# Two graph layers on one core: the second layer's first 21 gathers moved ahead of the first layer's last three groups

## The chip, the cores and the metric

The kernel runs on one core of a Trainium2 chip. The metric is the device time of one execution in microseconds (us); it was measured in three runs, and the median is given. Engines are named as in the profile: PE is TensorE (PEld its weight loads), DVE VectorE, ACT ScalarE, POOL GpSimd, SP SyncE; POOLq, ACTq and SPq are their instruction queues, which also issue DMAs.

## The reference

A graph has 6250 nodes with 256 features each and 106250 edges (a source, a destination, one of two relations), sorted by destination; each node also has an edge to itself. All is float32.

```python
# layer one
msgs = where(rel == r, edge_nn(x[src], W_rel[r], b_rel[r]))       # two dense layers with relu
agg = segment_sum(msgs, dst)
gates = agg @ W_ih.T + b_ih + b_hh
i, f, g, o = split(gates, 4)
hn = sigmoid(o) * tanh(sigmoid(i) * tanh(g))
x = layernorm(x + relu(relu(hn @ W1.T + b1) @ W2.T + b2) @ W3.T + b3)
# layer two: graph attention, 4 heads of 64
h = x @ W
e = leaky_relu(a_src[src] + a_dst[dst], 0.2)
alpha = exp(e - segment_max(e, dst)); alpha /= segment_sum(alpha, dst)
y = segment_sum(h[src] * alpha, dst) + bias + x
x = layernorm(x + relu(layernorm(y) * gamma + beta))
```

Layer two's gather of h[src] needs rows of h that layer one makes last, for any destination: that is the one barrier in the middle of the program.

## The kernel before

*Prelude.* The edge lists are read and packed so that self edges are left out (100000 edges stay), and turned into index tables: `idx0` and `idx1` hold, for each tile of 128 edges, the row that each lane gathers in layer one and in layer two. Beside this TensorE makes the messages of every node for both relations, which are stored in the table `parts0` (L1138 to L1179).

*Tiles, windows, groups.* The edges are 782 tiles of 128 (`TC`). Seven tiles are a window (`WT`, 112 windows, `NW`), whose destinations lie in at most 64 consecutive nodes (`SLOTS`); two windows are a group (56 groups, `NG`), which fills the 128 partitions with nodes. `low_i` and `low_b` hold the first node of each window.

*Layer one* (L1611 to L1675). A loop over steps n: step n issues the gather of one tile from `parts0` on POOL (`gather`, L1270, L1657) and, four steps later (`LAG`), the product that adds this tile into its group's sum in PSUM (`sum0`, L1621). What follows a sum, `turn` (L1433) and `update` (L1461), is written as generators; `Steps.step` (L1287) runs each up to its next `yield` once a step, so the order of instructions on every engine is fixed by hand, and a piece of group g stands on its engine behind the sums of later groups. `update` runs the gates and the three dense layers for four groups at a time, for single groups at the end (`quads`, L1310). It makes the row of layer two, `hr` (256 values of h and 4 logits, L1572), and stores it to `rows1` on SP (L1580); the last group's rows go there by a scatter on POOL (L1582). After the last step, `run.finish` (L1675) runs what is left.

*Layer two* (L1678 to L1975). A like loop: step t gathers one tile from `rows1` (L1946). Gathered tiles lie in ten buffers of seven tiles (`ring` "G", 10), which both layers share, so at most 70 tiles are ahead of their use. ACT copies the logits out (L1968, L1960); `weights` (L1751) then takes a pair of groups (single groups at the end) and finds maxima by transposing the logits on PE (L1766) and scanning them on DVE (L1773 to L1785); `weighted` (L1806) multiplies the rows by the exponentials (L1818), which frees a gather buffer; `sum1` (L1899) adds them up by one-hot products on PE (L1927); `finish` (L1825) normalizes and stores. `ahead` (L1699) loads a pair's tables on the ACT queue (L1708, L1715). The first pair's weights are started when tile 28 has come.

*Waits.* Each engine works its instructions in order. A gather waits until its buffer is free and, in layer two, until all stores to `rows1` have landed.

Of the kernel before, what the change touches and what calls it, by code (L numbers as in the profile page):

```python
# [42 lines left out]
P = 128  # L43
N = 6250
# [18 lines left out]
def blocks_of(n, size):  # L63
    return [(i, min(size, n - i)) for i in range(0, n, size)]
# [10 lines left out]
NC = -(-EC // CT)  # L75
HA = D + H
LAG = 4
SORTED = "the fast path runs only where the chip has found the edges sorted"


# [623 lines left out]
def gnn_kernel(  # L704
# [37 lines left out]
    rows1 = dram.tile([NP + P, HA], F32, name="rows1")  # L742
    slots = dram.tile([NW, (WT + 1) * P], BF16, name="slots")
    cuts = dram.tile([(NC + 1) * CT, P], F32, name="cuts")
    kept = dram.tile([NG, P, 3 * D], F32, name="kept")
    packed = dram.tile([2 * BLOCKS, HB], I32, name="packed")

# [19 lines left out]
    mark = const.tile([P, COLS], BF16, name="fmark")  # L767
    tail_i = const.tile([P, 1], I32, name="tail_i")
    tail_x = const.tile([P, 1], I32, name="tail_x")


    with (
# [15 lines left out]
        with (  # L788
# [257 lines left out]
            dstE = lp.tile([P, COLS], F32, name="dstE")  # L1046
            src0 = src1
            nc.vector.tensor_scalar(src0[:CT], src1[:CT], 1.0, None, op0=OP.subtract)
            for to, of in (
                (idx0, row),  # L1050
                (dstE, list_f[:, :, 1:]),
                (mark, rel_f[:, :, :P]),
                (idx1, src0),
                (first, steps),
            ):
                for k0, kn in blocks_of(NC, 4):
                    pt = lps.tile([P, 4 * CT], F32, name="turned")
                    for k in range(kn):
                        nc.tensor.transpose(
                            pt[:, k * CT : (k + 1) * CT], of[:CT, k0 + k, :], ident[:CT, :CT]  # L1060
                        )
                    n = min(kn * CT, COLS - k0 * CT)
                    if to is not mark:
                        nc.vector.tensor_copy(to[:, k0 * CT : k0 * CT + n], pt[:, :n])
                        continue

                    to2, of2 = (
                        ap.rearrange("p (g j) -> p g j", j=2 * WT)
                        for ap in (mark[:, k0 * CT : k0 * CT + n], pt[:, :n])
                    )  # L1070
                    for a, b, c in ((0, 1, 0), (1, 2, WT), (2, WT + 1, 1), (WT + 1, 2 * WT, WT + 1)):
                        nc.vector.tensor_copy(to2[:, :, a:b], of2[:, :, c : c + b - a])
# [50 lines left out]
            nc.vector.tensor_scalar(tail_x, tail[:, 0:1], float(NP - 1), None, op0=OP.min)  # L1123


            for w0, wn in blocks_of(NW, P // (WT + 1)):
                pt = lps.tile([P, 4 * CT], F32, name="turned")
                n = wn * (WT + 1)
                nc.tensor.transpose(
                    pt[:n, :P], slot[:, w0 : w0 + wn, :].rearrange("p w j -> p (w j)"), ident  # L1130
                )
                rel_b = lp.tile([P, P], BF16, name="rel_b", bufs=2)
                nc.scalar.copy(rel_b[:n, :], pt[:n, :P])
                nc.sync.dma_start(
                    slots[w0 : w0 + wn, :].rearrange("w (j e) -> (w j) e", e=P), rel_b[:n, :]
                )
# [51 lines left out]
    with tc.If(odd_v == 0) as cmp:  # L1188
        fast(
            tc, x, WihT, bih, bhh, W1T, b1, W2T, b2, W3T, b3, Wg, att_src, att_dst, bias, gamma,  # L1190
            beta, out, parts0, rows1, slots, cuts, kept, iota_f, iota_p, ident, idx0, idx1,
            first, mark, slot, low_i, tail_i, tail_x,
        )
    with cmp.Else():
        general(
# [6 lines left out]
def fast(  # L1202
# [32 lines left out]
    low_i,  # L1235
    tail_i,
    tail_x,
):

    nc = tc.nc  # L1240
# [27 lines left out]
        )[1]  # L1268

    def gather(to_tile, table, idx):  # L1270
        nc.gpsimd.indirect_dma_start(  # L1271
            out=to_tile,
            out_offset=None,
            in_=table,
            in_offset=bass.IndirectOffsetOnAxis(ap=idx, axis=0),
        )
# [24 lines left out]
    def half_of(w):  # L1301
        return slice(SLOTS * (w % 2), SLOTS * (w % 2 + 1))
# [20 lines left out]
    node3 = keep.tile([P, NG, 2, 3, 2 * H], BF16, name="node3")  # L1323
    nc.vector.memset(node3, 0.0)
    loop = keep.tile([P, NG, H], F32, name="loop")
    vec = keep.tile([P, 2, D], F32, name="fvec")
    eps_c = keep.tile([P, 1], F32, name="eps_c")
    nc.vector.memset(eps_c, EPS)
# [32 lines left out]
    def in_order(done, g):  # L1361
        if g != len(done):
            raise ValueError("groups are out of order")
        done.append(g)


    with (
# [32 lines left out]
        for k, v in enumerate((gamma, beta)):  # L1400
# [2 lines left out]
        nc.sync.dma_start(  # L1403
            rows1[N:, :].rearrange("(p r) f -> p (r f)", r=2),
            zero[: (NP + P - N) // 2, : 2 * HA],
        )

        run = Steps()
# [24 lines left out]
        def turn(g, i, ps, aT):  # L1433

            agg = ring(up, [P, D], F32, "agg", 3)

            kind = ring(up, [P, 2], F32, "kind", 3)
            for r in range(2):
                nc.vector.tensor_scalar(  # L1439
                    kind[:, r : r + 1], ps[:, D:], float(3 - r), None, op0=OP.is_equal  # L1440
                )
            for r, of in ((0, ps[:, :D]), (1, agg)):
                nc.vector.scalar_tensor_tensor(  # L1443
                    agg,
                    loop0[g][:, r * D : (r + 1) * D],
                    kind[:, r : r + 1],
                    of,
                    op0=OP.mult,
                    op1=OP.add,
                )  # L1450
            yield 1
            pt = ring(upp, [P, 4 * P], F32, "fpg", 5)[:, : 2 * P]
            for k in range(2):
                nc.tensor.transpose(  # L1454
                    pt[:, k * P : (k + 1) * P], agg[:, k * P : (k + 1) * P], ident
                )
            nc.vector.tensor_copy(  # L1457
                aT[:, :, i * P : (i + 1) * P], pt.rearrange("p (k n) -> p k n", k=2)
            )

        def update(groups, aT):  # L1461
            slow = min(3, max(1, (NG - 4 - groups[0]) // 4))
# [102 lines left out]
            for i, g in enumerate(groups):  # L1565
                u = everyone
                ph = ring(upp, [P, 4 * P], F32, "fpg", 5)[:, : D + 2 * H]
                for k in range(2):
                    nc.tensor.matmul(
                        ph[u, :], hs[i][:, k, u], Wx[:, k, :], start=(k == 0), stop=(k == 1)  # L1570
                    )
                hr = ring(up, [P, D + 2 * H], F32, "hr", 4)  # L1572
                nc.scalar.copy(hr[u, :], ph[u, :])  # L1573
                nc.scalar.copy(keep3[i][u, 2, :], ph[u, :D])

# [1 line left out]
                for w in windows_of(g):  # L1577
                    if w in at_w:
                        to = rows1[bass.ds(at_w[w], SLOTS), :]
                        nc.sync.dma_start(to, hr[half_of(w), :HA])  # L1580
                if g == NG - 1:
                    nc.gpsimd.indirect_dma_start(  # L1582
                        out=rows1,
                        out_offset=bass.IndirectOffsetOnAxis(ap=tail_i, axis=0),
                        in_=hr[:, :HA],
                        in_offset=None,
                    )
                yield 1
                nc.sync.dma_start(kept[g, u, :], keep3[i][u, :, :].rearrange("p c f -> p (c f)"))

# [53 lines left out]
        for n in range(TC + LAG):  # L1644
            if n < TC:
                g, t = order[n]
                k, turns = n % WT, n // WT // 10 % 2
                if k == 0:
                    seven = ring(rowsp, [P, WT * HA], F32, "G", 10).rearrange(
                        "p (j f) -> p j f", f=HA  # L1650
                    )
                    m = min(WT, TC - n)
                    of, to = mark[:, n : n + m, None], seven[:, :, D : D + 1]
                    nc.scalar.copy(to[:, ::-1, :][:, :m, :] if turns else to[:, :m, :], of)

                got[t] = seven[:, WT - 1 - k if turns else k, : D + 1]
                gather(got[t][:, :D], parts0, idx0[:, t : t + 1])  # L1657
                if t == order_of(g)[0]:
                    ohs[g] = ring(ep, [P, 2 * W8, SLOTS], F32, "oh0", 2)
                    one_hot(ohs[g], 2 * g, 2 * W8)  # L1660
                    loop0[g] = ring(up, [P, 2 * D], F32, "loop0", 2)
                    own_rows(g, lows_of(windows_of(g)), loop0[g], loops)
                    if g == NG - 1:
                        rows_x[g] = ring(up, [P, D], F32, "fxn", 8)
                        own_rows(g, {}, rows_x[g], x)
            if n >= LAG:
                g, t = order[n - LAG]
                if t != 2 * WT * g:
                    sum0(g, t, t == TC - 1)
                elif g:  # L1670
                    sum0(g - 1, t, True)
                if t == 2 * WT * g + WT:
                    sum0(g, 2 * WT * g)
            run.step()
        run.finish()  # L1675


    with (  # L1678
# [10 lines left out]

        nc.scalar.preload_act_table_set("natural_log_exp_and_others")  # L1690
        run = Steps()
        G, late = {}, []

        def tiles_in(g):

# [241 lines left out]
        run.start(aheads())  # L1937
        t = 0
        while t < TC + LAG or late or queue or run.chains:
            if t < TC:  # L1940
                w = t // WT
                if t % WT == 0:
                    G[w] = ring(rowsp, [P, WT * HA], F32, "G", 10).rearrange(
# [2 lines left out]
                gather(G[w][:, t - WT * w, :], rows1, idx1[:, t : t + 1])  # L1946
            k = t - LAG
            if 0 <= k < TC:
                w = k // WT
                g = w // 2  # L1950
                pair = pair_of[g]
# [86 lines left out]
```

## Time and profile before

| what | us |
|---|---|
| median of 3 runs | 2273.53 |
| lowest and highest | 2273.02, 2274.97 |
| profiled execution | 3062.77 |
| its span | 3061.0 |
| first gather of layer one | 203.84 |
| last gather of layer one, first of layer two | 1434.05, 1482.51 |
| last gather of layer two | 2969.30 |
| busy: PE, DVE, POOL | 1529.9, 1229.8, 1527.2 |
| one gather on POOL | 0.95 |

The profiled execution is 789 us longer than the timed runs, so its stretches cannot be read as stretches of these; what one operation takes, and what waits for what, can.

How to read the lines: a group of instructions gives line, engine, operation, what it writes and reads, and the count; after the first bar the busy time and the mean of one in ns; after the second the idle time of the engine before them and what ended most of it. A line of the order of time gives start, duration, engine, line, operation; in brackets the idle time of its engine before it, and what released it ("issue": nothing that the profile shows; "remote": a semaphore whose setter it cannot tell). A line of waits gives total us, times, and the longest. A line of stretches gives its length, the busy time and count for PE, PEld, DVE, ACT and POOL, and then the granted share of the PE clock, the DMA share and GB/s.

### The profile page before, as it was taken

Reading aid. Unit: us, or ns where it says so; the run is one execution under the profiler, and the core shown is the slowest. Engines: PE = TensorE matmul, PEld = TensorE weight load, DVE = VectorE, ACT = ScalarE, POOL = GpSimd, SP = SyncE. Lnnn points to the kernel's source line nnn. Section 1 sums busy time; section 2 is a strip of 40 time slices with the busy share of each in tenths; the row PEclk is TensorE's granted clock in tenths of the full one; section 3 lists DMA queues with packets and bytes.
Section 4 is the critical chain, followed back from the end, with each engine's and each line's share of the span. In section 5 each row is a group of like instructions: output and inputs, shape, how many; then the busy total and the mean of one; then the engine's idle time right before and its main releaser. Section 6 shows DMA issues by size and latency. Waiting matters only on the chain. (4 is left out here: it accounts for less than half of the span.)

```text
span 3061.0 us, 22029 instructions
## 1 busy us (share of the span) xinstructions
PE 1529.9 (50%) x5722; PEld 792.0 (26%) x5722; DVE 1229.8 (40%) x3333; ACT 506.0 (17%) x1526; POOL 1527.2 (50%) x1603
## 2 busy tenths in 40 slices
PE   9871276767676756788223332423324233242344
PEld 5540132323233322334111111212112121121222
DVE  8240132322333233333114544535445354453656
ACT  3320011211121211134201111111111111111112
POOL 0227566666666666641473354553545545455440
PEclk9985688878788878889555665656656566565667
DMA  4343334444444434442342243342433334243330
GB/s 150 109 137 108 96 104 122 143 124 139 132 139 135 131 118 132 131 127 79 100 117 79 80 116 86 103 108 81 117 84 106 105 83 117 82 111 100 88 99 27
DMA packets 163393, 332.53 MB, mean 109 GB/s; under 512 B 42451, under 2 KB 74290, under 8 KB 163257
## 3 DMA queue, kind: packets, MB, share of 16 engines
q0 software_dynamic: 75968, 208.00, 24.6%
q1 hardware_dynamic: 64736, 82.92, 8.4%
q10 hardware_dynamic: 22553, 40.12, 4.3%
q8 instruction: 47, 0.77, 0.1%
q14 instruction: 89, 0.73, 0.1%
HBM read 278.79 MB, written 52.12 MB: 108 GB/s over the span
## 5 line engine op out<-in xcount | busy, mean ns | idle before, releaser
L1271 POOL DMA_INDIRECT G<-rows,fidx x782 | 743.9, 951 | 746.6 <-DVE gw L1818 513.3
L1271 POOL DMA_INDIRECT G<-parts,fidx x782 | 752.3, 962 | 483.9 <-issue 216.4
L1927 PE MATMUL fps<-gw,oh 128*64 128x264 f32 (+1 forms) x1674 | 448.2, 480 | 284.1 <-DVE gw L1818 218.1
L1633 PE MATMUL fps<-G,oh 128*64 128x257 f32 (+1 forms) x1674 | 465.2, 428 | 91.5 <-issue 49.7
L1927 PEld LDWEIGHTS fps<-gw,oh 128*64 128x64 f32 (+1 forms) x1674 | 233.9, 171 | 468.6 <-DVE gw L1818 231.7
L1818 DVE TENSOR_TENSOR gw<-G,bank 128x1792 f32<-128x1792 f32 (+1 forms) x167 | 249.1, 1491 | 169.8 <-issue 123.7
L1633 PEld LDWEIGHTS fps<-G,oh 128*64 128x64 f32 (+1 forms) x1674 | 204.1, 152 | 332.1 <-issue 219.8
L1777 PE MATMUL turn<-s,toward 120*120 120x1 f32 (+2 forms) x60 | 15.7, 331 | 435.9 <-DVE s L1774 432.4
L1486 PE MATMUL fpg<-faT,fWihT 128*128 128x512 f32 (+2 forms) x432 | 182.9, 549 | 49.2 <-issue 28.7
L1773 DVE TENSOR_TENSOR_SCAN s<-cut,turn 120x128 f32<-120x128 f32 (+2 forms) x30 | 12.6, 419 | 448.1 <-remote 442.6
L1439 DVE TENSOR_SCALAR kind<-fps 128x1 f32<-128x1 f32 x112 | 12.4, 152 | 359.6 <-PE fps L1633 183.8
L1454 PE MATMUL fpg<-fident,agg 128*128 128x128 f32 x112 | 29.2, 351 | 236.7 <-DVE agg L1443 132.7
L1354 DVE TENSOR_TENSOR oh<-bank,fslot 128x1024 f32<-128x1024 f32 x112 | 136.1, 1215 | 0.6 <-ACT bank L1797 0.6
L1777 PEld LDWEIGHTS turn<-s,toward 120*120 120x120 f32 (+2 forms) x60 | 13.2, 278 | 450.2 <-DVE s L1774 445.9
L1766 PE MATMUL turn<-fident,e 128*120 128x128 f32 (+2 forms) x30 | 13.5, 449 | 229.3 <-issue 214.6
L1594 DVE COPY nd<-hr 128x4 f32<-128x4 f32 x56 | 9.8, 176 | 242.6 <-ACT hr L1573 150.4
L1486 PEld LDWEIGHTS fpg<-faT,fWihT 128*128 128x128 f32 x432 | 73.8, 198 | 124.0 <-issue 96.7
L1149 PE MATMUL fph<-fxc,fWrT 128*128 128x512 f32 (+1 forms) x208 | 91.7, 589 | 6.3 <-DMA fWrT<-in_WrT_dram 6.2
L1163 PE MATMUL fpm<-fWrT,fhT 128*128 128x256 f32 x392 | 89.1, 381 | 0.6 <-DVE fms L1171 0.5
L1867 ACT ACTIVATE frs<-fmv,eps_c 128x1 f32<-128x1 f32 x112 | 33.0, 294 | 332.0 <-DVE fmv L1866 121.9
L1457 DVE COPY faT<-fpg 128x256 f32<-128x256 f32 x56 | 23.6, 422 | 157.0 <-remote 72.6
L1779 ACT COPY ends<-turn 120x2 f32<-120x2 f32 (+2 forms) x30 | 4.8, 159 | 493.2 <-PE turn L1778 478.1
(237 smaller groups left out, 1964.7 us busy)
## 6 DMA issues: line engine op xcount, KB each, us to landing
kept<-keep SPq DMA_DIRECT2D x56, 384.0 KB
k<-kept ACTq DMA_DIRECT2D x56, 384.0 KB
dB<-slots ACTq DMA_DIRECT2D x112, 128.0 KB
loop<-parts SPq DMA_DIRECT2D x110, 128.0 KB
parts<-fms SPq DMA_DIRECT2D x49, 256.0 KB
G<-parts,fidx POOLq DMA_INDIRECT x782
G<-rows,fidx POOLq DMA_INDIRECT x782
rows<-hr SPq DMA_DIRECT2D x110, 65.0 KB
```

The lines of the kernel that those rows point to most:

```text
L1149: nc.tensor.matmul(ph[:, :cols], WrT_s[:, r, k, m * P : (m + 1) * P], xc[:, k, :cols], start=(k == 0), stop=(k == 1),)
L1163: nc.tensor.matmul(pm[:, r, :], hT[:, r, k, j * P : (j + 1) * P], WrT_s[:, r, k, :], start=(k == 0), stop=(k == 1),)
L1271: nc.gpsimd.indirect_dma_start(out=to_tile, out_offset=None, in_=table, in_offset=bass.IndirectOffsetOnAxis(ap=idx, axis=0),)
L1354: nc.vector.tensor_tensor(to[:, :nj, :], iota_s[:, None, :].to_broadcast([P, nj, SLOTS]), of[:, :, None].to_broadcast([P, nj, SLOTS]), op= ...
L1454: nc.tensor.transpose(pt[:, k * P : (k + 1) * P], agg[:, k * P : (k + 1) * P], ident)
L1457: nc.vector.tensor_copy(aT[:, :, i * P : (i + 1) * P], pt.rearrange("p (k n) -> p k n", k=2))
L1486: nc.tensor.matmul(pg[:, :cols], WihT_s[:, k, c * P : (c + 1) * P], aT[:, k, :cols], start=(k == 0), stop=(k == 1),)
L1633: nc.tensor.matmul(sums[g][to, :], ohj, got[t], start=begins, stop=ends)
L1777: nc.tensor.matmul(pd[:rs, 0:1], toward[:rs, 0, :rs], b[:, P - 1 : P], start=True, stop=True)
L1818: nc.vector.tensor_mul(gw[:, :, :D].rearrange("p j (h f) -> p j h f", h=H), of[:, :n, :D].rearrange("p j (h f) -> p j h f", h=H), ex[:, o ...
L1867: nc.scalar.activation(r, mv[u, k, 1:2], AF.Ln, bias=eps_c[u])
L1927: nc.tensor.matmul(sums[g][to, :], ohj, gw, start=begins, stop=ends)
```

## The change

The first 21 tiles of layer two (`EARLY`, three windows) are gathered before the rows of layer one's last three groups (`LATE`; windows 106 to 111) exist. In their index table, `idx_e`, a lane whose source is a node of these groups points at a row of zeros (`NOROW`). The missing rows are added later: the rows of the three groups stay in SBUF (`rows_l`), a one-hot of (node of partition p == source of edge) is made for each of the three groups over a window's 896 edges, and three products a tile give what is missing, which is added to the gathered tile (`complete`).

Order: 18 of the early gathers are issued behind layer one's last gather; they wait for the stores of group 52, and not for those of groups 53 to 55. Three more follow a small memset behind the last group's scatter. From tile 21 on, the gathers wait for all stores as before. In layer two's loop `complete(k)` stands at steps 4 to 24. The prelude gets the tables for this (`own_n`, `idx_e`, and `srcs` in DRAM, which is loaded to all partitions by three DMAs on the ACT queue). The rows of the last three groups in `rows1` are set to zero at the start of layer one. The ring `hr` has 3 buffers in place of 4.

```diff
@@ constants
+EARLY = 3 * WT
+LATE = 3
+NOROW = NP + SLOTS - 1
@@ gnn_kernel, prelude
             nc.vector.tensor_scalar(src0[:CT], src1[:CT], 1.0, None, op0=OP.subtract)
+            nc.sync.dma_start(srcs, src0[:EARLY, 0, :])
...
+            w0 = NW - 2 * LATE
+            held = lp.tile([P, LATE], F32, name="held")
+            for half, first_w, next_w in ((lo, w0, w0 + 1), (hi, w0 + 1, w0 + 2)):
+                o, v = own_n[half], held[half]
+                nc.vector.tensor_scalar(
...
+                nc.vector.tensor_tensor(
+                    v, o, low_b[half, next_w : next_w + 2 * LATE - 1 : 2], op=OP.is_lt
+                )
+                nc.vector.scalar_tensor_tensor(o, o, 1.0, v, op0=OP.add, op1=OP.mult)
+                nc.vector.tensor_scalar(o, o, 1.0, None, op0=OP.subtract)
+            before = lp.tile([P, EARLY], F32, name="before")
+            nc.vector.tensor_scalar(
+                before, idx1[:, :EARLY], low_b[:, w0 : w0 + 1], None, op0=OP.is_lt
+            )
+            early_f = lp.tile([P, EARLY], F32, name="early_f")
+            nc.vector.scalar_tensor_tensor(
+                early_f, idx1[:, :EARLY], float(-NOROW), before, op0=OP.add, op1=OP.mult
+            )
+            nc.vector.tensor_scalar(idx_e, early_f, float(NOROW), None, op0=OP.add)
@@ fast, start of layer one
+        for_late = N - 2 * LATE * SLOTS
+        nc.sync.dma_start(
+            rows1[for_late:N, :].rearrange("(p r) f -> p (r f)", r=4),
+            zero[: (N - for_late) // 4, : 4 * HA],
+        )
@@ fast, layer one
+        def gather_early(n):
+            for t in range(len(early), n):
+                w = t // WT
+                if t % WT == 0:
+                    G[w] = ring(rowsp, [P, WT * HA], F32, "G", 10).rearrange(
+                        "p (j f) -> p j f", f=HA
+                    )
+                e = gather(G[w][:, t - WT * w, :], rows1, idx_e[:, t : t + 1])
+                for store in rest:
+                    tc.declare_no_dep(e.ins, store.ins, reason="rows of other nodes")
+                for store in whole:
+                    tc.add_manual_dep(
...
-                hr = ring(up, [P, D + 2 * H], F32, "hr", 4)
+                hr = ring(up, [P, D + 2 * H], F32, "hr", 3)
+                if g >= NG - LATE:
+                    hr = rows_l[:, g - (NG - LATE), :]
...
+            if n == TC:
+                gather_early(EARLY - 3)
...
         run.finish()
+        nc.gpsimd.memset(pause, 0.0)
+        gather_early(EARLY)
@@ fast, layer two
+        srcb = []
+        for w in range(EARLY // WT):
+            srcb.append(ring(ep, [P, WT * P], F32, "srcb", 3))
+            nc.scalar.dma_start(srcb[w], at(srcs, w * WT * P, [[0, P], [1, WT * P]]))
+        def complete(t):
+            w, j = t // WT, t % WT
+            if j == 0:
+                srcb[w] = (srcb[w], ring(ep, [P, LATE, WT * P], F32, "ohS", 1))
+                for q in range(LATE):
+                    nc.vector.tensor_scalar(
+                        srcb[w][1][:, q, :], srcb[w][0], own_n[:, q : q + 1], None, op0=OP.is_equal
+                    )
+            more = ring(eps, [P, D + 2 * H], F32, "fps1", 2)[:, :HA]
+            for q in range(LATE):
+                nc.tensor.matmul(
+                    more,
+                    srcb[w][1][:, q, j * P : (j + 1) * P],
+                    rows_l[:, q, :HA],
+                    start=(q == 0),
+                    stop=(q == LATE - 1),
+                )
+            nc.vector.tensor_add(G[w][:, j, :], G[w][:, j, :], more)
...
-            if t < TC:
+            if EARLY <= t < TC:
...
             if 0 <= k < TC:
+                if k < EARLY:
+                    complete(k)
```

## The prediction

> **What bounds the kernel now.** I read the page's groups first, then GpSimd's waits, then the order of time around the change between the layers, then one steady period of layer two.
>
> ```profile
> L1271 POOL DMA_INDIRECT G<-rows,fidx x782 | 743.9, 951 | 746.6 <-DVE gw L1818 513.3
> L1271 POOL DMA_INDIRECT G<-parts,fidx x782 | 752.3, 962 | 483.9 <-issue 216.4
> ```
>
> Each layer has 782 gathers on POOL. One takes 0.95 us and the next starts 0.30 us later, 1.2525 us from start to start where nothing is waited for: 980 us a layer.
>
> ```profile
> 1434.05 0.95 POOL L1271 DMA_INDIRECT G<-parts,fidx  x1 [0.30 <-issue]
> 1478.75 1.00 POOL L1582 DMA_INDIRECT rows<-hr,tail_i  x1 [43.75 <-ACT keep L1574]
> 1482.51 0.97 POOL L1271 DMA_INDIRECT G<-rows,fidx  x1 [2.75 <-issue]
> 1483.78 0.95 POOL L1271 DMA_INDIRECT G<-rows,fidx  x1 [0.30 <-issue]
> ```
>
> Between the layers POOL stands idle: 43.75 us until the last group's rows exist, then 2.75 us until they have landed. This is the hole that the change fills.
>
> ```profile
> 1434.55 3.54 SPq L1580 DMA_DIRECT2D rows<-hr  x2
> 1452.05 2.92 SPq L1580 DMA_DIRECT2D rows<-hr  x2
> 1469.27 2.45 SPq L1580 DMA_DIRECT2D rows<-hr  x2
> ```
>
> These are the row stores of groups 52, 53 and 54. The early gathers wait for the first pair only.
>
> ```profile
> POOL G L1271 <- DVE gw L1818: 513.3, 25, 42.7
> POOL loop L1271 <- DMA loop<-parts: 60.5, 1, 60.5
> ```
> ```profile
> 2028.93 0.95 POOL L1271 DMA_INDIRECT G<-rows,fidx  x1 [19.84 <-DVE gw L1818]
> 2014.76 0.42 DVE L1773 TENSOR_TENSOR_SCAN s<-cut,turn 120x128 f32<-120x128 f32 x1 [18.96 <-remote]
> 2046.56 0.42 DVE L1818 TENSOR_TENSOR gw<-G,bank 128x256 f32<-128x256 f32 x1 [4.94 <-issue]
> ```
> ```profile
> 2014.70:2050.60 35.90, 17.78 (x80) 10.04 (x81) 26.78 (x68) 6.26 (x28) 16.48 (x18) 0.69 0.37 102
> 2014.70:2069.20 54.50, 18.05 (x82) 10.17 (x82) 26.78 (x69) 6.85 (x28) 26.66 (x28) 0.63 0.36 99
> ```
>
> In the profiled execution layer two is not paced by its gathers. A pair of groups (28 tiles) takes 54.45 us, while 28 gathers take 35.07. Once a pair VectorE stands 18.7 us before a scan that waits for TensorE, and POOL then waits 19.6 us for a buffer. In the rest, 35.75 us, VectorE is busy 26.8.
>
> **The profiled execution against the median.** It took 3062.77 us (span 3061.0 and 1.8 around it), the timed runs 2273.53. The difference, 789, is near to the sum of such stalls: 513 and 60.5 above, some 190 of shorter POOL waits in layer one (its 784 gathers take 1230 us instead of 982, less the 60.5). So I take the timed run as the profile without these stalls, and add it up. To the first gather 203.8. To layer one's last gather 783 x 1.2525 = 980.7. To layer two's first: landing 3.0, last product 0.9, the last group's chain 23.2 (from its first VectorE step at 1455.5 to POOL's at 1478.75), then 3.8: 31. I call this moment T0, 1215.5. From here two sums are possible.
> Paced by gathers: 781 x 1.2525 = 978.2 to the last gather; 3.9 to the last group's scan; 16.4 because from the last pair's scan to the last group's the trace takes 82.8 us and 53 gathers only 66.4; 37.5 from that scan to the end. 2251.5 + 1.8 = 2253, 20 below the median.
> Paced by VectorE at 35.75 a pair: first scan at T0 + 38.6, 25 periods of 35.75, 82.8, 37.5: 2268 + 1.8 = 2270, 4 below.
> Both leave room for some lag at the end of layer one, which no view gives without the stalls. So the gathers bound layer one and the hole for certain; in layer two the gathers and VectorE's chain lie within 2% of each other. That decides the case.
>
> [...] the seventh gather of layer two ends at 1490.98, the copy that needs it starts at 1493.06, 2.1 us later. [...] DMA is 0.43 busy in 1500 to 1600, where gathers run at full rate, so there is room. [...] The trace grants 0.88 in 1250 to 1400 and 0.55 in 1500 to 1600.
>
> **The change, part by part.**
> *Early gathers.* 18 follow the last gather of layer one at once: group 52's chain is issued at step 767, 14 steps before the last gather, so its rows have landed. They fill 18 x 1.2525 = 22.5 us of the hole. On POOL the last group's scatter is queued behind them; it is due 27 us after the last gather, so it has 3 to 4 us of cover; were the chain 6 us shorter, the scatter and all after it would come some 3 us late. Three more gathers (3.8 us) and a memset lie where POOL waited 2.75 us for the landing. Gather 21 starts at T0 + 1.4, where gather 0 had started at T0: 26.3 - 1.4 = **24.9 us won on POOL**.
> *Prelude.* 11 small VectorE operations at 0.15 us (tail_x: 0.144; 64x1 adds 0.136 to 0.151), 1.7 us; TensorE has idle time there (12.8 busy of 20 us in 140 to 160, VectorE 16.8), so VectorE is the late one and I count all of it. Bounds 0 and 3. The store of srcs is one more issue on SP, some 0.4 us among others.
> *Layer one.* A zero store of 399 KB on SP ahead of the first own-row loads (152 KB: 0.47 us of issue at 213.0). Those are first read after 14 gathers and 4, 22 us later, so: nothing; uncovered, some 3 us. The hr ring of 3: nothing in the trace, where the copies come 5 us apart; without the stalls a quad's fourth may wait 1 us for a store, hidden by 70 tiles of gathered lead.
> *Products.* 21 x 3 products of 128x128 by 260 columns, two records each. The nearest row is the product that makes hr:
>
> ```profile
> 1424.96 1.16 PE L1569 MATMUL fpg<-Wx,fyT 128*128 128x264 f32 x4
> ```
>
> Four records, with the next work 0.99 later, 0.247 each: 126 x 0.247 = 31 us; 47 us at the 0.55 clock of 1500 to 1600 instead of some 0.83. I take 31[...]. VectorE makes 9 one-hots of 128x896 (0.61 to 1.07 by rows of that shape) and 21 additions (0.42, the 128x256 one from PSUM): 14 to 19 us, beside TensorE save some 1.3 us a window, because the one-hots have one buffer and wait for the window before. ScalarE issues 3 loads of 459 KB ahead of the pair's own (0.6 us each); the first lands at about T0 + 3.5. Products end at 4.3 + 31 + 3 + 2.6 = **T0 + 41** (T0 + 57 at the low clock). Queued behind them are the transpose and scan of pair 0, which stood at T0 + 38.6: now T0 + 42 (to 58).
> *What is late next.* Before, pair 1's scan was due with its data at T0 + 73.7. From the first scan to the second VectorE is busy 22.8 us instead of 26.8, some 31 with its idle time, so pair 1 comes at T0 + 73 (to 89). Its data are there at T0 + 48. The first buffer that POOL needs again (gather 70, T0 + 62.8) comes free at about T0 + 60. So POOL has its 24.9 us, and VectorE starts where it started before. The gain arrives at the end only as far as VectorE's own pace Y catches up, in 25 periods: 25 x (35.07 - Y), at most 24.9.
>
> **The cases.**
> *Gathers pace layer two (0.47).* For: the ledger holds without any fault of layer two; of VectorE's 35.75 some 9 us is idle, 4.9 of it behind six DMA issues of ScalarE, and 1 us less is enough. Against: the 20 us left over. With Y at 34.2, 21.7 of the 24.9 arrive; less 1.7 of prelude: 20 us, 2253.5. Alone this case spans 2248 (all of it, no prelude) to 2268 (Y at 34.9).
> *VectorE paces it, products at full clock (0.22).* The hole is filled for nothing: pair 1 at the old place, 1.7 us of prelude: 2275, from 2270 to 2278.
> *Slower: VectorE paces it and the products run long (0.27).* TensorE throttled, products to T0 + 57: first scan 20 us late, of which some 4 come back in the shorter first period, 16, and 1.7: 2291; half of that at a clock between, 2283. It decides from where the products end after T0 + 42 and Y is over 35.07. For: 0.55 in that stretch, and Y = 35.75 in the trace. [...]
> *The early gathers wait all the same (0.04),* for a store that comes late: only the landing wait goes, 2.75 less 1.7: 2272.
>
> **Numbers.** Forecast 2253.5. Two in ten lie outside 2248 to 2284. Faster by over 0.2% (4.5 us, about what a measurement of this kernel can tell from no change): 0.48; within: 0.20; slower: 0.32.
>
> **What would show it.** Gap between layers: 18 gathers at 1.25 us right after layer one's last, the scatter no later than before. In the profile of the changed kernel the stall before the scans will be there again, so its span says little of layer two's pace. Products: 126 records within some 35 us, pair 0's scan at about T0 + 42. Wrong if the timed gain is under 5 us with the hole filled: then VectorE's chain paced layer two.

## The result, and the profile after

The changed kernel takes 2273.49 us (median of 12 runs, 2271.42 to 2277.64), the kernel before 2274.77 us beside it (12 runs); the ratio is 0.9994, 95% interval 0.9985 to 1.0002. The 20 us of the forecast are not there: no difference that can be measured. The rival "VectorE paces it, products at full clock" (2275, 2270 to 2278) is what happened.

On five of the six chips of the experiments below the kernel before takes some 3050 us in every run (3034.66 to 3080.33), and the profiles there show slowed stretches, in which TensorE stands and VectorE waits before a scan once a pair, as in the profile of before (18.7 us there, 18.4 in b_again); on the sixth it takes 2275.77 (2270.20 to 2279.82). So each experiment is compared with runs of before on its own chip, and that time tells the kind of chip.

The changed kernel's own profile is of the 2274 kind: span 2272.9 us. The order of time on POOL around the seam between the layers:

```profile
1191.80 0.95 POOL L1311 DMA_INDIRECT G<-parts,fidx  x1 [0.30 <-issue]
1193.05 0.95 POOL L1311 DMA_INDIRECT G<-rows,idx_e  x1 [0.30 <-issue]
1221.04 1.00 POOL L1669 DMA_INDIRECT rows<-rows_l,tail_i  x1 [5.35 <-ACT keep L1661]
1222.34 0.96 POOL L1311 DMA_INDIRECT G<-rows,idx_e  x1 [0.19 <-issue]
1226.11 0.95 POOL L1311 DMA_INDIRECT G<-rows,fidx  x1 [0.30 <-issue]
```

The hole is filled. Eighteen early gathers follow layer one's last one without a wait, the scatter is still held by ScalarE's last copy (5.35 us of idle time), three more follow, and gather 21 starts at 1226.11. GpSimd has its 25 us. Where they are at the end, the waits tell (total us, times, longest):

```profile
POOL out_dram L2004 <- ACT fy L1991: 72.4, 1, 72.4
POOL G L1311 <- DVE gw L1936: 6.7, 10, 0.8
DVE gw L1936 <- ACT gw L1935: 167.8, 150, 5.2
ACT gw L1935 <- DMA dB<-slots: 103.3, 25, 4.5
ACT e L2088 <- DMA G<-rows,fidx: 4.6, 11, 0.4
```

GpSimd hardly waits for buffers (6.7 us). Its last gather starts at 2187.33, and then it stands 72.4 us before the last rows can be stored: from that gather to the end of the span it is 85.6 us, where the ledger of a layer paced by its gathers had 57.8. The third line shows what VectorE waits for: ScalarE. The fourth shows what held ScalarE 25 times, some 4 us each: its own issues of the `dB` loads. The last shows that it hardly waited for gathered rows. One such wait in the order of time (ACTq is ScalarE's queue issuing DMAs), the scans around it, and then one pair of groups later in the layer (a stretch: length; busy us and count of PE, PEld, DVE, ACT, POOL; PE clock, DMA share, GB/s):

```profile
1291.21 2.47 ACTq L1826 DMA_DIRECT2D dB<-slots  x4
1293.71 1.82 ACTq L1833 DMA_DIRECT2D cut<-cuts  x2
1295.58 0.16 ACT L1935 COPY gw<-bank 128x4 f32<-128x4 f32 x1 [4.17 <-DMA dB<-slots]
1295.77 0.42 DVE L1936 TENSOR_TENSOR gw<-G,bank 128x256 f32<-128x256 f32 x1 [4.88 <-ACT gw L1935]
1299.72 0.42 DVE L1891 TENSOR_TENSOR_SCAN s<-cut,turn 120x128 f32<-120x128 f32 x1
1335.30 0.41 DVE L1891 TENSOR_TENSOR_SCAN s<-cut,turn 120x128 f32<-120x128 f32 x1
```
```profile
1900.00:1935.80 35.80, 18.26 (x82) 10.20 (x82) 26.79 (x69) 6.85 (x28) 26.79 (x28) 0.67 0.55 150
```

Six DMA issues take 4.3 us of ScalarE's time; its small copy of four columns stands behind them, and VectorE's product needs the copy and waits 4.88 us. From the fourth scan to the 25th (1371.78 to 2123.9, 21 periods) a pair takes 35.8 us, 26.8 of them busy on VectorE. The gathers need 35.07. The 18.7 us stall before the scans, which the prediction expected to see again, is in no pair of this trace.

The head of layer two: the last addition, and what stands between it and the first scan.

```profile
1263.45 0.42 DVE L1810 TENSOR_TENSOR G<-G,fps 128x260 f32<-128x260 f32 x1 [0.89 <-PE fps L1803]
1263.91 2.46 ACTq L1826 DMA_DIRECT2D dB<-slots  x4
1266.42 1.82 ACTq L1833 DMA_DIRECT2D cut<-cuts  x2
1268.63 0.19 ACT L2080 COPY e<-G 128x4 f32<-128x4 f32 x1
1269.38 0.42 DVE L1891 TENSOR_TENSOR_SCAN s<-cut,turn 120x128 f32<-120x128 f32 x1 [0.39 <-PE turn L1884]
```

The products end at 1263.9. Then the same six issues, of the next pair, come before ScalarE's last copy of logits: 4.3 us more.

### The profile page after: what moved, and what is told of

Its sections match the earlier page's. It is cut to its first block, busy times and chain, and to the rows that moved or that the text cites. A ratio compares the mean times of both kernels' runs of the same rounds, so it can differ in the third digit from the quotient of the medians.

```text
span 2272.9 us, 22263 instructions
## 1 busy us (share of the span) xinstructions
PE 1579.8 (70%) x5848; PEld 796.0 (35%) x5848; DVE 1253.1 (55%) x3374; ACT 506.9 (22%) x1526; POOL 1526.0 (67%) x1604
## 4 chain that ended last, share of the span: by engine, by line
DVE 27%; POOL 20%; PE 18%; issue 15%; DMA 13%; ACT 4%; ACTq 2%; DVEq 0%; SPq 0%; another core or an unknown queue 0%; POOLq 0%
POOL G L1311 20%; DVE gw L1936 7%; PE fps L1721 5%; DMA G<-parts,fidx 5%; PE fpg L1571 4%; DVE oh L1396 3%; DMA packed<-frame,place 2%; DMA dB<-slots 2%; PE fpm L1200 2%; PE fpg L1654 2%; DVE fst L1983 2%; ACTq L1826 2%; DMA G<-rows,fidx 2%; PE fps L1803 1%; PE fps L2045 1%
## 5 line engine op out<-in xcount | busy, mean ns | idle before, releaser
L1311 POOL DMA_INDIRECT G<-rows,fidx x761 | 727.1, 955 | 235.4 <-issue 210.2
L1721 PE MATMUL fps<-G,oh 128*64 128x257 f32 (+1 forms) x1674 | 529.2, 431 | 142.6 <-DMA G<-parts,fidx 127.5
L2045 PE MATMUL fps<-gw,oh 128*64 128x264 f32 (+1 forms) x1674 | 429.0, 465 | 237.3 <-DVE gw L1936 237.3
L1721 PEld LDWEIGHTS fps<-G,oh 128*64 128x64 f32 (+1 forms) x1674 | 195.9, 150 | 449.3 <-DMA G<-parts,fidx 229.9
L1936 DVE TENSOR_TENSOR gw<-G,bank 128x1792 f32<-128x1792 f32 (+1 forms) x167 | 249.0, 1491 | 169.6 <-ACT gw L1935 167.8
L1571 PE MATMUL fpg<-faT,fWihT 128*128 128x512 f32 (+2 forms) x432 | 171.9, 522 | 0.2 <-DVE faT L1507 0.2
L1985 ACT ACTIVATE frs<-fmv,eps_c 128x1 f32<-128x1 f32 x112 | 33.0, 295 | 327.4 <-DVE fmv L1984 167.8
L938 POOL DMA_INDIRECT packed<-frame,place x21 | 20.9, 994 | 109.0 <-DVE fms L1208 71.5
L1991 ACT ACTIVATE fy<-fy,frs 128x256 f32<-128x256 f32 x112 | 67.2, 600 | 98.3 <-DVE gw L1930 52.9
L1200 PEld LDWEIGHTS fpm<-fWrT,fhT 128*128 128x128 f32 x392 | 73.4, 190 | 17.9 <-issue 4.7
L1935 ACT COPY gw<-bank 128x28 f32<-128x28 f32 (+1 forms) x167 | 28.4, 170 | 228.8 <-DMA dB<-slots 103.3
L1654 PE MATMUL fpg<-Wx,fyT 128*128 128x264 f32 x224 | 76.9, 473 | 3.0 <-ACT fyT L1645 3.0
```

Source lines behind the costliest of these rows:

```text
L1200: nc.tensor.matmul(pm[:, r, :], hT[:, r, k, j * P : (j + 1) * P], WrT_s[:, r, k, :], start=(k == 0), stop=(k == 1),)
L1311: return nc.gpsimd.indirect_dma_start(out=to_tile, out_offset=None, in_=table, in_offset=bass.IndirectOffsetOnAxis(ap=idx, axis=0),)
L1571: nc.tensor.matmul(pg[:, :cols], WihT_s[:, k, c * P : (c + 1) * P], aT[:, k, :cols], start=(k == 0), stop=(k == 1),)
L1654: nc.tensor.matmul(ph[u, :], hs[i][:, k, u], Wx[:, k, :], start=(k == 0), stop=(k == 1))
L1721: nc.tensor.matmul(sums[g][to, :], ohj, got[t], start=begins, stop=ends)
L1936: nc.vector.tensor_mul(gw[:, :, :D].rearrange("p j (h f) -> p j h f", h=H), of[:, :n, :D].rearrange("p j (h f) -> p j h f", h=H), ex[:, o ...
```

## Experiments

**Theory.** VectorE's chain, 35.8 us a pair with ScalarE's issues in it, paces layer two in both kernels. (For the kernel before this stays an inference: no trace of it comes from a chip of the 2274 kind.) The early gathers only let GpSimd run ahead of it; the products hold the second scan near where it was due (T0 + 74.9 for T0 + 73.7), and the 25 us are handed back in the tail. **Rival 1:** the gathers pace it, and something else lost the gain again. **Rival 2:** the head alone is late, and the chain has room to spare afterwards.

### The pairs' loads issued by SyncE (four runs of the changed kernel)

```diff
-                    nc.scalar.dma_start(
+                    nc.sync.dma_start(
                         dB[half_of(w), :, :].rearrange("p j e -> p (j e)"),
...
-                nc.scalar.dma_start(
+                nc.sync.dma_start(
                     cut[i * GS * H : (i * GS + n) * H, :],
```

> The changed kernel with a pair's six table loads issued by SyncE instead of ScalarE. Theory 1: VectorE's wait of 4.9 us a pair for ScalarE's copy, which stands behind these six issues, goes or shrinks; VectorE's own pace falls under the gathers' 35.07 and the gathers take over: 18 to 24 us faster, 2250 to 2256, with 4 us of that from the head, where the same issues hold the first logits. Rival 1: the gathers already pace it: within 3 us of 2273. If only the head's 4 us come: 2269, and the wait was not in VectorE's chain.

> The changed kernel with a pair's six table loads issued by SyncE. On a chip without the slowed stretches (2274 us for before), theory 1: VectorE's part of a pair is 31.4 us as the slowed traces show it, the gathers pace layer two at 35.07, and the 25 us that they gained reach the end: 2235 to 2256. Rival 1: within 3 us of 2273. With the slowed stretches: 0.5 to 1.0% slower than before, as twice measured.

On a chip of the 2274 kind (a_sploads4): 2239.19 us (4 runs) beside 2275.77 for before, ratio 0.9841, 0.9820 to 0.9863: **36.6 us faster**. Waits, order of time and stretches of that trace:

```profile
DVE gw L1936 <- ACT gw L1935: 63.7, 155, 2.1
ACT e L2088 <- DMA G<-rows,fidx: 216.5, 73, 5.3
POOL out_dram L2004 <- ACT fy L1991: 41.4, 1, 41.4
```
```profile
1265.79 0.19 ACT L2080 COPY e<-G 128x4 f32<-128x4 f32 x1
1266.39 0.42 DVE L1891 TENSOR_TENSOR_SCAN s<-cut,turn 120x128 f32<-120x128 f32 x1 [0.60 <-PE turn L1884]
1323.62 0.42 DVE L1891 TENSOR_TENSOR_SCAN s<-cut,turn 120x128 f32<-120x128 f32 x1
1355.07 0.41 DVE L1891 TENSOR_TENSOR_SCAN s<-cut,turn 120x128 f32<-120x128 f32 x1
1625.31 0.21 ACT L2088 COPY e<-G 128x28 f32<-128x28 f32 x1 [4.16 <-DMA G<-rows,fidx]
1626.43 0.16 DVE L1988 SCALAR_TENSOR_TENSOR frs<-fmv,frs 128x1 f32<-128x1 f32 x1 [2.68 <-ACT frs L1986]
```
```profile
1331.40:1362.80 31.40, 17.54 (x82) 9.93 (x82) 26.64 (x69) 6.67 (x29) 23.78 (x26) 0.72 0.58 158
1900.00:1935.20 35.20, 18.02 (x82) 10.13 (x82) 26.85 (x68) 6.89 (x28) 26.67 (x29) 0.66 0.56 152
```

VectorE's work a pair is the same (26.6 to 26.9 us busy). Its wait for ScalarE falls from 167.8 to 63.7 us in all, and the early pairs come every 31.5 us: the chain is now faster than the gathers and catches up. Counted with the same zero, the second scan is 7.6 us earlier than in the changed kernel, the eighth 29.2. From the ninth on a pair takes 35.3 us, VectorE waits 2 to 3 us a pair for ScalarE (the 1626.43 line), and ScalarE has waited 4.16 us for gathered rows (the 1625.31 line; 216.5 us in all, where the changed kernel had 4.6): the gathers set the pace. The last gather is at 2182.84, only 4.5 us earlier than in the changed kernel, and the tail behind it is 54.5 us in place of 85.6: 4.5 + 31.1 = 35.6, the difference of the two spans. That is the theory with its place and its size; both rivals are out, for GpSimd's work was not touched, and most of the gain comes after the head.

On the chips of the 3050 kind the same kernel gave 3076.46 (ratio to before 1.0100, 1.0063 to 1.0138), 3072.89 (1.0070, 1.0040 to 1.0100; run a_sploads2, expected as the first) and 3075.21 (1.0064, 1.0041 to 1.0088; a_sploads3, likewise). No gain over the changed kernel, and the section on the slowed chips shows why.

### The same move in the kernel before

> The kernel before with the same move of the six loads to SyncE. Theory 1: layer two becomes gather-paced here too, so the ledger of the gathers holds: 15 to 18 us faster than before, 2256 to 2259; the early gathers are then worth at most 25 us less the prelude beyond that, and only as far as VectorE's chain goes under 35.07. Rival 1: within 3 us of 2274.

3047.08 us (ratio 0.9992, 0.9972 to 1.0013), then 3045.73 (b_sploads2: 0.9998, 0.9978 to 1.0018) and 3047.65 (0.9995, 0.9973 to 1.0016), all on chips of the 3050 kind, where a pair stays at 54.4 to 54.5 us. For the third the expectation was:

> The kernel before with a pair's six loads issued by SyncE, for a chip where before takes 2275. Theory 1: VectorE's part of a pair falls to 31.5, the gathers pace from the first pair on (35.1 to 35.3), and the time is that of the changed kernel with the same move (2239) plus the 24.9 us that the early gathers win on GpSimd, less 1.7 of prelude: 2260 to 2264, 12 to 15 us under before. Rival 1 (the move alone is what helps, the early gathers bring nothing in any case): 2239 as well.

It found such a chip too. So how the 36.6 us divide between the move and the early gathers was not measured where it matters. An estimate from the traces: with the gathers pacing, the 24.9 us that GpSimd wins come off the end one for one, less at most some 1 us of prelude, so the move alone would stand near 2263, some 12 under before, and the early gathers would bring the other 24.

### GpSimd made slower

```diff
+                if t % (4 * WT) == 6:
+                    for _ in range(6):
+                        nc.gpsimd.memset(rest_p, 0.0)
```

> The changed kernel with six small memsets on GpSimd after every 28th gather of layer two, from tile 34 on, some 6 us without gathers, placed a few gathers after TensorE's first work for the next pair's scan. If TensorE's slowed stretch lasts until the gathers stop (as the traces suggest: it ends 4 to 5 us after GpSimd runs out of buffers), it now ends at this pause: VectorE's stall before the scan falls from 18.7 to about 8 to 11 us, a pair from 54.4 to 44 to 47, and the kernel is some 180 to 250 us faster, 2820 to 2890, though GpSimd does more. If the stretch has a length of its own, the pause lies in GpSimd's 19.5 us of waiting and nothing changes, 3071. On a chip without slowed stretches the gathers and the pause would take 41 us a pair and pace layer two: 2400.

The diff leaves out the line that makes the tile `rest_p`. The chip was of the 2274 kind: 2393.36 us (one run) beside 2275.77.

```profile
1611.26 0.41 DVE L1891 TENSOR_TENSOR_SCAN s<-cut,turn 120x128 f32<-120x128 f32 x1
1652.34 0.41 DVE L1891 TENSOR_TENSOR_SCAN s<-cut,turn 120x128 f32<-120x128 f32 x1
1656.27 6.18 POOL L2068 MEMSET rest_p<- 128x1024 f32 x6
1662.61 0.95 POOL L1311 DMA_INDIRECT G<-rows,fidx  x1 [0.15 <-issue]
```

27 pauses of 6.2 us are 167 us of GpSimd's time; the kernel is 120 slower than the changed kernel, and once GpSimd's lead is used up, from the sixth pair on, a pair takes 41.1 us, which is 28 gathers and a pause. So some 47 us of GpSimd's time could be lost before it set the end: about the lead of the early gathers, 25, and 0.7 us for each of 27 pauses, 19. In the changed kernel GpSimd paces nothing in layer two. (TensorE's stall, which the expectation was about, does not occur on this chip; its last sentence, for this kind of chip, came out.)

### Without the products, and with fewer of them

```diff
-                if k < EARLY:
-                    complete(k)
```

> The changed kernel without the added rows: its one-hots, its 63 products and its 21 additions at the head of layer two are left out, so the rows of the last three groups are missing from the first 21 tiles. The early gathers stay. Theory 1 (VectorE's chain paces layer two, and the head of the chain stands behind the products): the first pair's scan comes about 28 us after gather 18 to 21 were free to go, that is near 1240 in place of 1269, the second near 1275 in place of 1299, later periods stay 35.8, and the time falls by about 25 us to 2248. Rival 1 (gathers pace layer two, the products only lie beside them): at most 3 us faster, 2270. Rival 2 (only the head is late, the chain has room to spare afterwards): the first scans come early, but the later ones come back to the gathers' 35.1 a pair and the gain is 3 to 15 us.

3030.24 us, ratio to before 0.9929 (0.9904 to 0.9953); once more (a_noprod2) 3039.89, 0.9946 (0.9921 to 0.9971). For the second the expectation was, for a chip of the other kind:

> The changed kernel without the added rows (one-hots, 63 products and 21 additions at the head are left out, so the rows of the last three groups are missing from the first 21 tiles), ScalarE's issues where they were. Theory 1: the chain keeps 35.8 us a pair but starts earlier: second pair's scan near 1275 in place of 1299.5, and the time is about 25 us less, 2246 to 2252. Rival 2 (only the head is late, the chain has room to spare): the later scans do not move, 2265 to 2273.

```diff
-EARLY = 3 * WT
+EARLY = 2 * WT
```

> The changed kernel with 14 early tiles in place of 21, so 42 products in place of 63 and 6 one-hots in place of 9. Without TensorE's slowed stretches: theory 1 says that the first scan is no longer held by the products (two windows end at about T0 + 28) but by tile 27 and the loads, near T0 + 30, and the chain starts some 8 to 12 us earlier than in both kernels: 2262 to 2266; rival 1 (gathers pace) says 8 us less than the 21 tiles give, so nothing gained or 5 us slower. With the slowed stretches: theory 1 says a third of the cost of the products comes back, 10 to 20 us faster than the changed kernel, 3052 to 3060.

3062.30, ratio 1.0006 (0.9982 to 1.0030); once more (a_early14_2) 3058.96, 1.0025 (1.0003 to 1.0047), with:

> The changed kernel with 14 early tiles in place of 21 (42 products), ScalarE's issues where they were. Theory 1: the head ends earlier with a third less products and the chain with it, at an unchanged 35.8 us a pair: 8 to 12 us faster than with 21, 2262 to 2266. If the gathers paced it: 9 us slower than with 21, 2282.

And the changed kernel itself beside them:

> The changed kernel once more, now beside the runs of before whose layer two stands 18.7 us a pair before its scans (54.4 us a pair). Theory 1 (VectorE's chain, whatever it waits for, paces layer two, and the gathers won are handed back in a longer tail): not faster here either; with a pair at 54.4 the early gathers are worth nothing and the products at the head stand under the slowed TensorE, so 15 to 30 us slower, 3065 to 3080. Rival 1 (the gathers' 25 us reach the end): 20 us faster, 3030.

3071.12, ratio 1.0085 (1.0058 to 1.0113): **on a chip of this kind the change is slower**, which the third case of the prediction had for a slowed TensorE. The products stand under the slowed TensorE: the order of time from the first one-hot to the last addition, with a hole in the middle.

```profile
1487.77 1.88 DVE L1797 TENSOR_SCALAR ohS<-srcb,own_n 128x896 f32<-128x896 f32 x3 [5.67 <-DMA srcb<-srcs]
1547.68 2.97 PE L1803 MATMUL fps<-rows_l,ohS 128*128 128x260 f32 x6 [34.84 <-issue]
1580.13 0.42 DVE L1810 TENSOR_TENSOR G<-G,fps 128x260 f32<-128x260 f32 x1 [0.89 <-PE fps L1803]
```

92.8 us in place of the 35.5 on the other kind of chip (1228.40 to 1263.87). TensorE stands 45.9 of these us in two gaps, of 11.04 and 34.84, that the profile ties to no wait, and the granted clock over the whole stretch is 0.66, against 0.94 on the other kind of chip. Without the products the early gathers gain 0.5 to 0.7% there, some 16 to 22 us. The second scan, counted from layer one's last gather, tells where: 199.4 and 199.5 us in the two traces of the kernel before, 189.8 and 190.5 without the products, 213.8 in a_again. So some 9 us of the gain and 14 of the loss lie at the head of VectorE's chain, and the rest is not placed. Against the runs without products all 63 cost 1.4 to 1.6%, and the version with 42 of them 0.8%. The head is where the theory puts the price; its size on a 2274 chip was not measured, so a version with 14 tiles is not shown to be better there.

With both edits, 14 tiles and the loads on SyncE:

> Both at once: 14 early tiles, and the pairs' loads issued by SyncE. Without TensorE's slowed stretches (2274 us for before), theory 1: VectorE's part of a pair is 31.4 us, the gathers pace layer two at 35.07, and 14 early tiles are worth 16 us on GpSimd: 2240 to 2252. Rival 1: within 3 us of the changed kernel. With the slowed stretches (3050 for before): the period stays 54.4, since the stretch fills what ScalarE gives up, and the time is that of the 14 tiles alone, within 0.4% of before.

3067.90, ratio 1.0019 (1.0002 to 1.0036); once more 3058.84, 1.0016 (0.9999 to 1.0034): the 14 tiles alone, as expected of a 3050 chip. The second was to show whether fewer early tiles turn from a gain into a loss once the gathers pace; that stays open:

> 14 early tiles and the pairs' loads issued by SyncE. Theory 1: with VectorE's part at 31.5 the gathers pace, and now 7 early tiles less cost 7 x 1.25 = 8.8 us: 2246 to 2250, while the same 7 tiles less were a gain where ScalarE issues the loads. If the head still set the end: 2230 to 2236.

### The slowed chips: what sets a pair there

The kernel before, profiled again:

> The kernel before, profiled again. If its profile falls near the timed 2274 us this time, it says where its layer two stood. Theory 1 (VectorE's chain paces layer two in both kernels): scans of successive pairs 35.7 to 35.9 us apart, second pair's scan at the same distance from layer one's last gather plus the hole as in the changed kernel (within 3 us of 1299.5), and the time from the last gather to the end well over 60 us. Rival 1 (gathers pace it): scans 35.1 us apart, and POOL's gathers without waits for buffers.

3048.97 us, scans 54.4 us apart: not the expected period of either theory, since the stall of the first profile of before is there again. Its waits, and those of the kernel before with the loads on SyncE (b_sploads2):

```profile
DVE s L1773 <- remote: 441.2, 24, 18.7
```
```profile
DVE s L1773 <- remote: 529.0, 23, 23.5
```

ScalarE gave up its 4.9 us there too (no such wait is left in a pair), and the stall before the scan grew from 18.7 to 23.1: the pair stays at 54.4. What goes with it shows on GpSimd's side of b_again:

```profile
2050.94 0.95 POOL L1271 DMA_INDIRECT G<-rows,fidx  x1 [0.30 <-issue]
2057.21 0.42 DVE L1773 TENSOR_TENSOR_SCAN s<-cut,turn 120x128 f32<-120x128 f32 x1 [18.59 <-remote]
2071.38 0.95 POOL L1271 DMA_INDIRECT G<-rows,fidx  x1 [19.48 <-DVE gw L1818]
```

The scan comes 5.3 us after GpSimd has run out of buffers. In the fifteen traces of this kind that make all of layer two's sums, of before and of changed kernels, with and without the move, the median of that distance lies between 5.3 and 5.7 us. So a pair is 28 gathers (34.8 from the first start to the last end), 5.3 until the scan, 14.2 from there until a buffer is free: 54.3, whatever ScalarE does.

Two kernels left out most of layer two's sums: of a group's products only the first, the shared one and the last ones are made, so the sums lack the other tiles.

```diff
-            nc.tensor.matmul(sums[g][to, :], ohj, gw, start=begins, stop=ends)
+            if begins or ends or j == WT:
+                nc.tensor.matmul(sums[g][to, :], ohj, gw, start=begins, stop=ends)
```

> The changed kernel with most of layer two's sums on TensorE left out: of the 14 products of a group only the first, the shared one and the two last are made, so the sums lack the other tiles. VectorE's, ScalarE's and GpSimd's work is all there. If the stall of 18.7 us a pair is a slowed TensorE, it shrinks or goes, and what paces layer two can be read: theory 1 says scans 35.8 us apart then, POOL waiting for buffers that VectorE frees; rival 1 says 35.1 apart with POOL never waiting; if TensorE's sums themselves were in the chain, the period falls under 35 in VectorE's part.

> The kernel before with the same sums left out. Theory 1: the same 35.8 us a pair as the changed kernel with these sums left out, second pair's scan at the same distance from layer one's last gather within 5 us, and the same distance from there to the end: the early gathers change only how long POOL stands idle at the end. Rival 1: the end comes 20 us later in this kernel than in the other, counted from layer one's last gather.

2984.81 and 2955.75 us (one run each) beside 3051.70. The expectation of 35.8 failed: the pairs are 51.6 apart in both, VectorE's stall is divided (7.2 us before the reduction of `pn`, 7.9 before the second scans) and shrinks from 18.7 to 15.1, and it ends 4.8 us after the gathers stop. So most of it doesn't come from these sums. The ends were not the same either: counted from layer one's last gather the changed one is 32 us later, and 31.5 of that are there at the third scan, behind its slowed products.

Whether the stop of the gathers frees TensorE, or both have one cause, is open: the pause on GpSimd was meant to tell, and met a chip without the stall.

## Why the prediction was wrong

**The step that failed: "Gathers pace layer two (0.47) ... With Y at 34.2, 21.7 of the 24.9 arrive".** The trace gave Y, VectorE's own pace, as 35.75; I argued it down by 1.55 because some of its 9 us of idle time might go. Nothing in the change touched that idle time. In the changed kernel the pace was 35.8, over the gathers' 35.07, and 25 x (35.07 - Y) is then nothing. The text had named the right part (4.9 us behind six DMA issues) and the right sign ("1 us less is enough"): with the issues moved Y was 31.5, and the gain came. (The case's far end is also mis-summed: Y at 34.9 gives 25 x 0.17 less 1.7, so 2271 and not 2268.)

**The 20 us left over** between the ledger of the gathers and the timed run were taken as room in layer two. Some 9 of them lie ahead of it in the changed kernel: T0, the scatter and the 3.76 us behind it, is at 1224.8 in place of 1215.5, with 0.9 before the first gather (204.73), 6.4 more in layer one's gathers (987.1 for 980.7) and 2.0 in the hole (33.0 for 31). The other 11 would be VectorE's slower pace, if the kernel before stood alike. An estimate with the changed trace's figures fits: T0 without the 0.9 at 1223.9, the scan 38.6 later as before, 25 x 35.8, then 77.7 from the last pair's scan to the last group's, 37.6 and 1.8 make 2274.6, where the estimate for gathers that pace is 2263.

**Steps that held.** 18 gathers at 1.25 us right behind layer one's last; scatter with cover left; gather 21 at T0 + 1.3; 25 us won on GpSimd. Products: one-hots to last addition 35.5 us, ending at T0 + 39.1 for T0 + 41; in the last window a tile's six records took 1.31 us, 0.22 each, and the waits for a new window's one-hots were 1.5 and 1.1 us; the granted clock was 0.94 over these 35.5 us, 0.80 in the first 11.6 and 1.00 after them. The 3 us that T0 + 41 has beside 4.3, 31 and 2.6 were an estimate of mine; the first window's first addition came 3.00 us behind its first record and the second 1.80 later, where the second window has 2.00 and 1.32, so some 1.5 were slower. Prelude: the first gather is 0.9 us later than in the profile of before, but traces of before differ by 1.5 there (203.8 to 205.3), so the 1.7 can't be told. "pair 0's scan at about T0 + 42": T0 + 44.6; "pair 1 comes at T0 + 73": T0 + 74.9. The distance between the two scans was to be 31: 30.3.

**A term that was missing:** the six issues of the second pair's loads stand between the products and ScalarE's last copy of logits: 4.3 us, of which 2.6 show between T0 + 42 and T0 + 44.6, because the products ended 1.9 us early. With them on SyncE the first scan came 4.2 us earlier, counted from layer one's last gather.

**"The stall before the scans will be there again"** was wrong: it goes with the chip, not with the program. On a chip that has it the change is slower (0.85%), as in the third case, and products run long, 92.8 us where that case had taken up to 53. But the cause is not the one it named: it had the products slowed by a low clock, and of the 57.3 us more than on the other kind of chip 45.9 are the two gaps in which TensorE does nothing; its busy time grew by 5.7. The sign of being wrong came: under 5 us with the hole filled, so VectorE's chain paced layer two.

## What to carry to other kernels

Work won on an engine counts only where that engine has the longest period (here 25 us of GpSimd, with 35.07 us a pair beside VectorE's 35.8, left the time where it was: 2273.49 for 2274.77); when two periods lie within 2%, take the measured ones as they are, and ask for the change that makes the slower one shorter, here a queue of DMA issues in front of a copy that another engine waits for. An engine that runs ahead gives its gain back in the tail (85.6 us behind the last gather here, and 54.5 once VectorE kept up): compare the time from its last instruction to the end before and after. And when a profile and the timed runs differ by a third, find out which stalls belong to the chip before reading a pace from it.

## What the runs showed of the hardware

- **DMA issues took time of the engine that issued them.** Six of them took 4.3 us of ScalarE in the 1291.21 and 1293.71 lines, 0.6 us for one of `dB` and 0.9 for one of `cut`. With the issues on SyncE, ScalarE's copy and VectorE behind it no longer stood 4 to 5 us a pair: the longest such wait of VectorE fell from 5.2 us (changed kernel) to 2.1 (a_sploads4).
- **One program, two kinds of chip: 2274 and 3050 us.** On the slow kind TensorE's records have a hole in each pair: in layer two of the profile of before there are 22 ahead of the first product behind the scans (L1777), 15.6 to 19.6 us long and most of them 19.3; b_again has 19.28 and 19.22 in the same place. With the loads on SyncE VectorE's wait before the scan is 23.0 us on average (b_sploads2, 529.0 us in 23). In those 22 holes of before 42 of SyncE's 77 register instructions (MOVE, FUSED_REGOPS) take more than 0.5 us, most of these 0.7, and the others 0.03 to 0.04 save one of 0.41; in the changed kernel's trace none takes more than 0.06. The trace of before also holds 4,101 landing marks of GpSimd's 1,589 DMAs, that of the changed kernel 25,227 for as many. Fewer marks and the holes stand together in these two traces; what causes the holes is not shown.
